# A Perceiver layer on one core: the last key's projection and stores moved, the time mixing's exponentials first, other banks for the last attention output

## The chip, the core and the metric

The kernel runs on one core of a Trainium2 chip, in one launch. A core has a matrix engine (TensorE; PE in the profile, PEld for its weight loads), a vector engine (VectorE, DVE), a scalar engine (ScalarE, ACT), GpSimd (POOL) and SyncE (SP), which issues this kernel's DMAs. Each engine takes its instructions in order; semaphores order them across engines. The metric is the device time of one execution in microseconds (us), lower is better. Times are medians of several runs; one execution is recorded by the profiler.

## What is computed

All values are float32. `x` is [32, 64, 256]: 32 samples, 64 queries of 256 values. `ctx` is [32, 1601, 192]: 1601 context rows, so 1601 keys, in each sample. The layer is

```python
# cross attention, 16 heads of 64
xn = layernorm(x)
q  = heads(xn @ w_q)                 # [32, 16, 64, 64]
k, v = heads(ctx @ w_kv)             # [32, 16, 1601, 64] each
p  = softmax(q @ k.T / 8)            # over the 1601 keys
x  = x + heads_joined(p @ v) @ w_out + b_out
# time mixing, per sample over its 64 queries
xn = layernorm(x); s = xn moved by one query
k, v, r = (xn*m + s*(1-m)) @ W.T     # three mixes m, three weights Wk, Wv, Wr
td = exp(-exp(time_decay)); e = exp(time_first + k)
wkv_t = (num + e_t v_t) / (den + e_t);  num = td num + exp(k_t) v_t;  den = td den + exp(k_t)
x  = x + (sigmoid(r) * wkv) @ Wo.T + bo
# feed forward
x  = x + relu(layernorm(x) @ w1 + b1) @ w2 + b2
```

The last line stands for the feed-forward part, which the change does not touch.

## The kernel before

**Folding.** Keys and values of the 1601 rows are never formed. Each head's query is folded with its part of `Wk`, so that a score is the product of a folded query (192 values) and a context row. The weighted sum of context rows is taken first and projected with `Wv` afterwards. Of the 1601 keys, 1536 lie in 12 blocks of 128, the next 64 are the rest block, and the last one (number 1600, the "odd" key) is handled by itself.

**Setup stage** (0 to about 142 us). `Wk` is transposed head pair by head pair (`wkT_ps`, L399 and L400). Then four groups `tg` of eight samples follow. Each group is worked in two halves `e` of eight heads: the queries (`q_ps`, L282, copied with the scale by ScalarE to a slice of `room[1]`), the folded queries' first 128 values (`ql_ps`, L300, and `q_lo`, L307) and their last 64 (`qh_ps`, L322). They are stored to `q_dram` (L310, L336). The odd key's context rows `codn` are transposed to `cod` (`cod_ps`, L217) and projected to all heads (`kod_ps`, L224, copied to `kodT`) once, behind the second half of the first group. `odd_scores` (L242) makes that key's scores after both halves of each group, and four small stores for each half send them to `o_dram` (L254). Their source is `od`: for the first half a tile that borrows the memory of `m2` (named `spare`), for the second a slice of `room[1]`.

**Memory that is used twice.** `room[0]` and `room[1]` are the two buffers of the tag `s_sb`. In the setup stage they hold weights and queries; later they hold the scores of the half batches in turn. `room[0]` becomes the scores of u = 0 and `room[1]` those of u = 1. The tile `m2` becomes the running maximum of the scores.

**Half batches.** After the setup 64 half batches follow, u = 0 to 63: sample b and half j of its heads, 512 columns (8 heads of 64 queries). For each u:

- for j = 0 the rest block's scores (`rest_ps`, L616, copied at L627), with the odd key's row read back from `o_dram`;
- the scores: 72 matmuls into six tiles `s_ps` of two PSUM banks (L639), ScalarE copies each tile to `s_sb` (L646), VectorE forms the maximum `m` (L648, L650), GpSimd takes it over the partitions (`mb`, L663);
- `av_lo` and `av_hi` of the half batch before: `o_lo` (48 matmuls at L449) and `o_hi` (48 at L847), begun and ended by the rest block's `left` (L797, L807), in PSUM banks with the tags `o_lo` and `o_hi`;
- `exps(u)`: `left` first (VectorE subtracts the maximum from `rest` at L671, ScalarE takes the exponential at L672, and SP stores the odd key's row of it to `pd_dram`), then three parts of four blocks (L682, L683);
- `total` and `inverse` of the denominators (`t` L759, GpSimd's `den` L762, VectorE's `turned` L774 and `rden`), and `out`, which multiplies `o_lo` and `o_hi` by them into `oT_lo` and `oT_hi` (L868, L873).

**Other work in between.** Every four half batches complete two samples, 128 rows, which is one of 16 tiles i. With phase = (u - 5) % 4: phase 0 projects to values (`Out.vproj`; it also multiplies the odd key's weights with its values, `odd`, L895, whose inputs SP loads as `odd_pd`), phase 1 projects the output (`yproj`) and norms, phase 2 mixes (`mix`), and phase 3 does the time mixing's projections. A dictionary `fill` puts such work behind a matmul c of `av_lo`: in phase 3 `project` stands behind c = 3 and `gate` behind c = 9.

```python
elif phase == 3 and i >= 0:
    fill = {3: [mixer.project], 9: [mixer.gate]}
```

`project` makes `Wk_ps` and `Wv_ps` on TensorE and then, on ScalarE, `ek` (L533) and two instructions `e` (L535); `gate` makes `Wr_ps`. All three go by a helper whose line is L449. In u = 3 the same place holds the odd key's values for all samples (`odd_values`: `vod`, L704 and L712), its outputs (`odd_outs`: `u_ps`, L723), and `decay`.

**What sets the order.** A scheduler orders each engine's instructions by the program's order and by `tc.issue_after(x)`, which holds what is issued under it until instruction `x` stands in the order. The DMAs' order on SP is decided in the same way, and each DMA issue waits for the DMA that was issued eight before it. Behind the last group's stores, SP loads for u = 0 the `rest` rows, `rows`, the second sample's `cb`, folded queries `q`, the first sample's context `c` (L143), and then `late_loads` (`wv_lo` and the other weights, from L419).

Of the kernel before, what the change touches and what calls it, by code (L numbers as in the profile page):

```python
# [9 lines left out]
F32 = mybir.dt.float32  # L10
# [10 lines left out]
def kernel(  # L21
# [104 lines left out]
    with ExitStack() as st_b:  # L126
        with ExitStack() as st_a:
# [83 lines left out]
                    copied = nc.vector.tensor_copy(xnT[:, c, :], pt)  # L211
                return xnT, copied

            def last_keys(codn, wk_lo, wk_hi, kodT, sps):

                pc = sps.tile([P, 2, B], F32, tag="ps", name="cod_ps")
                nc.tensor.transpose(pc[:, 0, :], codn[:, 0:P], ident[0:B, 0:B])  # L217
                nc.tensor.transpose(pc[0:C2, 1, :], codn[:, P:C], ident[0:B, 0:B])
                nc.vector.tensor_copy(cod[:, 0, :], pc[:, 0, :])
                nc.vector.tensor_copy(cod[0:C2, 1, :], pc[0:C2, 1, :])  # L220
                pk = sps.tile([P, NP, B], F32, tag="ps", name="kod_ps")
                for n, w, rs in ((0, wk_lo, slice(0, P)), (1, wk_hi, slice(0, C2))):
                    for hp in range(NP):
                        nc.tensor.matmul(  # L224
                            pk[:, hp, :],
                            lhsT=w[:, hp * P : (hp + 1) * P],
                            rhs=cod[rs, n, :],
                            start=(n == 0 and hp == 0),
                            stop=(n == 1),
                            skip_group_check=True,  # L230
                        )
                nc.vector.tensor_copy(kodT, pk)

            def odd_scores(tg, e, kodT, qTs, od, sps):

                po = [
                    sps.tile([P, TG], F32, tag="f", name=f"odd_ps_{tg}_{e}_{o}", bufs=6)
                    for o in range(2)
                ]
                for k in range(4):  # L240
                    for o in range(2):
                        nc.tensor.matmul(  # L242
                            po[o][k * B : (k + 1) * B, :],
                            lhsT=kodT[o * HD : (o + 1) * HD, 4 * e + k, :],
                            rhs=qTs[k // 2][o * HD : (o + 1) * HD, k % 2, :],
                            start=True,
                            stop=True,
                        )
                nc.vector.tensor_copy(od[:, 0, :], po[0])
                nc.scalar.copy(od[:, 1, :], po[1])  # L250
                for k in range(4):
                    r0 = k * B + tg * QB
                    h0 = 8 * e + 2 * k
                    nc.sync.dma_start(  # L254
                        o_dram[tg][h0 : h0 + 2].rearrange("o b n -> b o n"), od[r0 : r0 + QB]
                    )

            def queries(tg, xnT, copied, sp, sps, wq_sb, wkT, room, kodT, codn, wk_lo, wk_hi, spare):

                more = tg + 1 < B // QB
                following = None, None
                all_q = []
                for e in range(NP // 4):
                    if e == 0 and more:
                        with tc.issue_after(copied.ins):
# [3 lines left out]
                    for g in (2 * e, 2 * e + 1):  # L272
                        slot = (tg * NP // 2 + g) % 5
                        qT = room[1][:, slot * 2 * TG : (slot + 1) * 2 * TG].rearrange(
                            "p (k t) -> p k t", k=2
                        )
                        qTs.append(qT)
                        for k in range(2):
                            hp = 2 * g + k
                            pq = sps.tile([P, TG], F32, tag="ps", name=f"q_ps_{tg}_{hp}")  # L280
                            for c in range(2):
                                nc.tensor.matmul(  # L282
                                    pq,
                                    lhsT=wq_sb[:, c, hp * P : (hp + 1) * P],
                                    rhs=xnT[:, c, :],
                                    start=(c == 0),
                                    stop=(c == 1),
                                )
                            nc.scalar.activation(qT[:, k, :], pq, AF.Copy, scale=HD**-0.5)
                    if e == 1 and more:  # L290
                        following = turned_x(tg + 1, xn, sp, sps)
                    for g, qT in zip((2 * e, 2 * e + 1), qTs):
# [21 lines left out]
                    all_q.append(qTs)  # L314
# [19 lines left out]
                    for n in range(2):  # L334
# [2 lines left out]
                            q_dram[tg][:, P:C, ns].rearrange("b p n -> p b n"),  # L337
                            hi[n * C2 : (n + 1) * C2].rearrange("p b h t -> p b (h t)"),
                        )
                    if e == 1 and tg == 0:  # L340
                        last_keys(codn, wk_lo, wk_hi, kodT, sps)
                    if e == 1:
                        for n in range(2):
                            odd_scores(tg, n, kodT, all_q[n], spare[n], sps)
                return following, store

            def ctx_prep(b):
# [12 lines left out]
            with tc.tile_pool(name="setup", bufs=1) as sp, tc.tile_pool(  # L360
# [19 lines left out]
                wkT = wkT.rearrange("p (h c) -> p h c", c=C)  # L380
                wqr = w_q.rearrange("(c p) n -> p c n", p=P)
                halves = [slice(n * INNER // 2, (n + 1) * INNER // 2) for n in range(2)]
                for n, ns in enumerate(halves):
                    nc.sync.dma_start(wk_lo[:, ns], w_kv[0:P, ns])
                    nc.sync.dma_start(wk_hi[:, ns], w_kv[P:C, ns])
                    if n == 0:
                        nc.sync.dma_start(x_sb[:, 0:2, :], xr[:, 0:2, :])
                        nc.sync.dma_start(x_sb[:, 2:4, :], xr[:, 2:4, :])
                for ns in halves:
                    nc.sync.dma_start(wq_sb[:, :, ns], wqr[:, :, ns])  # L390
                for n in range(4, NT, 4):
                    nc.sync.dma_start(x_sb[:, n : n + 4, :], xr[:, n : n + 4, :])
                nc.sync.dma_start(codn, ctx_768[:, NK - 1, :])
                b_tiles = {0: blocks_load(0)}
                for g in range(NP // 2):
                    ps = sps.tile([P, 2, C], F32, tag="ps", name=f"wkT_ps_{g}")
                    for k in range(2):
# [3 lines left out]
                            ps[:, k, P:C], wk_hi[:, hp * P : (hp + 1) * P], ident[0:C2, 0:C2]  # L401
                        )
                    nc.scalar.copy(wkT[:, 2 * g : 2 * g + 2, :], ps)

                turned = turned_x(0, normed_x(0, sp), sp, sps)
                for tg in range(B // QB):
                    turned, store = queries(tg, *turned, sp, sps, wq_sb, wkT, room, kodT, codn, wk_lo, wk_hi, spare)
# [69 lines left out]
            class Mixing:  # L477
# [48 lines left out]
                def project(self):  # L526
# [5 lines left out]
                    self.e = rp.tile(shape, F32, tag="e", name=f"e_{i}")  # L532
                    nc.scalar.activation(self.ek, pk, AF.Exp)  # L533
                    for c in range(2):
                        nc.scalar.activation(  # L535
                            self.e[:, c], pk[:, c], AF.Exp, bias=cols[:, 1, c : c + 1]
                        )
                    self.ekv = rp.tile(shape, F32, tag="in_v", name=f"ekv_{i}")
# [199 lines left out]
            class Half:  # L738
# [85 lines left out]

                def av_lo(self, fill, behind):

                    self.po = ps_o.tile([P, HALF], F32, tag="o_lo", name=f"o_lo_{self.u}")
                    self.ph = ps_o.tile([P, HALF], F32, tag="o_hi", name=f"o_hi_{self.u}")[:, 0:HH]
# [50 lines left out]
            class Out:  # L879
# [7 lines left out]
                def vproj(self):  # L887
# [6 lines left out]
                    self.odd = rp.tile([ODD, P], F32, tag="odd", name=f"odd_{i}")  # L894
                    nc.vector.tensor_tensor(self.odd, odd_pd[:, 0], odd_pd[:, 1], ALU.mult)  # L895
                    pv = [bank([P, 2, 2, P], f"v_ps_{i}_{r}") for r in range(2)]
                    for r in range(2):
                        for j in range(2):
# [24 lines left out]
                                    )  # L923
                    for r in range(2):
                        nc.scalar.copy(self.outT[:, :, r], pv[r])

                def yproj(self):
                    i = self.i
# [20 lines left out]
            for u in range(2 * B):  # L949
# [12 lines left out]
                    turned_w = []  # L962
                elif u == 3:
                    fill = {
                        3: [lambda: vods.append(odd_values())],
                        6: [lambda: odd_outs(vods[0])],
                        9: [lambda: decay(top)],
                    }
                    vods = []
                elif phase == 1 and i >= 0:  # L970
                    fill = {2: [out.yproj], 6: [older.out] if i else []}
                elif phase == 2 and i >= 0:
# [5 lines left out]

                    hooks = {3: parts[0:2], 4: parts[2:3], 5: parts[3:]}
                elif last is not None:  # L980
                    hooks = {3: [last.inverse]}
                    last.total()
                else:
                    hooks = {}
# [9 lines left out]
                if last is not None:  # L994
                    last.av_lo(fill, done)
                parts = exps(u, s_sb, rests[j], mb)
                with tc.issue_after(turned_w[-1].ins) if u == 2 else ExitStack():
                    for part in parts if u else ():
                        part()
                if u == 1:  # L1000
# [30 lines left out]
            last.out()  # L1031
            older.scan()
            out.vproj()
            out.yproj()

        NB = 4
# [128 lines left out]
```

## Time and profile before

| | us |
|---|---|
| median of 3 runs | 2641.41 |
| range of the runs | 2638.94 to 2643.0 |
| the profiled execution's own time | 2641.73 |
| its span (first to last instruction) | 2639.9 |
| TensorE busy in it | 2576.9 |
| VectorE busy | 1928.4 |
| ScalarE busy | 984.6 |
| GpSimd busy | 409.7 |

The mean granted clock of TensorE in that execution is 0.986 of full speed. The profile names instructions by engine, line and tile; in the lists of waits, the columns are the total in us, the number of times, and the longest. In the timelines, the first number is the start from the span's beginning and the second the length; the bracket at the end gives the idle time just before and what ended it. In the tables of windows there follow for each stretch the length, the busy time of each engine (with the number of instructions), the granted clock, the share of the DMA engines and GB/s.

### The profile page before, as it was taken

How to read it: one execution, taken by the hardware profiler on the slowest of the kernel's cores; microseconds unless marked ns; L12 is line 12 of the kernel's file. 1: busy time of each engine (PE TensorE's matmuls, PEld its weight loads, DVE VectorE, ACT ScalarE, POOL GpSimd, SP SyncE). 2: the span in 40 equal slices, each digit the busy share in tenths (PEclk: the TensorE clock that was granted, in tenths of full speed). 3: DMA queues.
4: the chain of work that ended last, by engine and by line, in shares of the span. 5: the costliest groups of instructions: out<-in, count | busy, mean ns of one | idle time of the engine just before them, and what ended most of it. 6: DMA issues, size and time to landing. Idle time of an engine off the chain costs nothing.

```text
span 2639.9 us, 38243 instructions
## 1 busy us (share of the span) xinstructions
PE 2576.9 (98%) x15650; PEld 1236.6 (47%) x15650; DVE 1928.4 (73%) x2363; ACT 984.6 (37%) x1104; POOL 409.7 (16%) x372
## 2 busy tenths in 40 slices
PE   8989999999999999999999999999999999999999
PEld 4334444444444444444444444444444444444466
DVE  4466777878787878878787878878787878787631
ACT  2343334434333434333433334343343334343221
POOL 1001111111111111111111111111111111111100
PEclk9999999999999999999999999999999999999999
DMA  7885332333232223233233222323332322310100
GB/s 175 233 211 82 73 65 45 64 64 63 53 64 57 53 51 64 46 64 64 54 63 61 58 50 53 65 45 65 64 61 55 64 56 50 55 45 2 51 11 22
DMA packets 435968, 174.24 MB, mean 66 GB/s; under 512 B 334960, under 2 KB 421520, under 8 KB 435792
## 3 DMA queue, kind: packets, MB, share of 16 engines
q1 hardware_dynamic: 435792, 171.79, 31.6%
q8 instruction: 123, 2.02, 0.3%
q14 instruction: 53, 0.43, 0.1%
HBM read 141.07 MB, written 29.10 MB: 64 GB/s over the span
## 4 chain that ended last, share of the span: by engine, by line
PE 66%; DVE 14%; issue 11%; POOL 4%; ACT 3%; SPq 2%; DMA 1%; DVEq 0%; POOLq 0%; ACTq 0%
PE s_ps L639 27%; PE o_lo L449 14%; PE o_hi L847 8%; DVE s_sb L682 4%; DVE m L650 3%; PE y_ps L449 2%; PE q_ps L282 2%; DVE t L759 2%; PE h_ps L1076 2%; PE fy L1090 2%; POOL mb L663 2%; POOL den L762 2%; PE ql_ps L300 1%; DVE cT L355 1%; PE v_ps L902 1%
## 5 line engine op out<-in xcount | busy, mean ns | idle before, releaser
L639 PE MATMUL s_ps<-q,cT 64*128 64x512 f32 x4608 | 1006.6, 591 | 3.7 <-ACT rest L627 2.3
L449 PE MATMUL o_lo<-s_sb,c 128*64 128x512 f32 x3072 | 709.6, 609 | 6.8 <-DMA c<-in_ctx_dram 6.8
L639 PEld LDWEIGHTS s_ps<-q,cT 64*128 64x128 f32 x4608 | 442.2, 187 | 535.6 <-issue 518.2
L646 ACT COPY s_sb<-s_ps 128x1024 f32<-128x1024 f32 x384 | 388.5, 1012 | 732.8 <-PE s_ps L639 731.1
L682 DVE TENSOR_TENSOR s_sb<-s_sb,mb 128x2048 f32<-128x2048 f32 x192 | 431.5, 2283 | 0.0
L683 ACT ACTIVATE s_sb<-s_sb 128x2048 f32<-128x2048 f32 x192 | 367.3, 1914 | 124.3 <-DVE s_sb L682 124.3
L449 PEld LDWEIGHTS o_lo<-s_sb,c 128*64 128x64 f32 x3072 | 218.5, 140 | 403.9 <-issue 399.6
L650 DVE TENSOR_TENSOR m<-m,s_sb 128x1024 f32<-128x1024 f32 x256 | 312.3, 1220 | 47.7 <-ACT s_sb L646 27.1
L847 PE MATMUL o_hi<-s_sb,c 128*64 128x256 f32 x3072 | 342.8, 379 | 0.0
L759 DVE TENSOR_TENSOR t<-t,s_sb 128x1024 f32<-128x1024 f32 x256 | 311.9, 1218 | 8.7 <-DVE rstd_ln L110 0.4
L847 PEld LDWEIGHTS o_hi<-s_sb,c 128*64 128x64 f32 x3072 | 222.3, 137 | 139.2 <-issue 38.4
L762 POOL PARTITION_ALL_REDUCE den<-t x64 | 207.1, 3236 | 387.3 <-issue 365.9
L774 DVE STREAM_TRANSPOSE turned<-den 128x512 f32<-128x512 f32 x64 | 45.5, 711 | 274.5 <-POOL den L762 274.5
L672 ACT ACTIVATE rest<-rest 128x512 f32<-128x512 f32 x64 | 40.4, 631 | 504.8 <-DVE rest L671 485.7
L663 POOL PARTITION_ALL_REDUCE mb<-m x64 | 114.2, 1785 | 469.2 <-DVE m L656 414.9
L671 DVE TENSOR_TENSOR rest<-rest,mb 128x512 f32<-128x512 f32 x64 | 44.3, 692 | 108.4 <-POOL mb L663 108.4
L604 POOL MEMSET rest<- 64x256 f32 x128 | 39.3, 307 | 428.7 <-issue 192.9
L355 DVE STREAM_TRANSPOSE cT<-cb 128x768 f32<-128x768 f32 x96 | 89.5, 957 | 9.0 <-DMA cb<-in_ctx_dram 9.0
L797 PE MATMUL o_lo<-rest,rows 64*128 64x256 f32 x256 | 82.8, 404 | 4.2 <-DVE oT_lo L868 4.2
L648 DVE TENSOR_TENSOR m<-s_sb 128x1024 f32<-128x1024 f32 x64 | 76.2, 1191 | 12.1 <-DMA o_dram<-spare 12.0
L807 PE MATMUL o_hi<-rest,rows 64*128 64x256 f32 x256 | 83.0, 405 | 0.0
L111 POOL TENSOR_TENSOR rstd_ln<-rstd_ln,root 128x1 f32<-128x1 f32 (+1 forms) x24 | 32.1, 1337 | 313.0 <-DVE rstd_ln L110 287.3
(156 smaller groups left out, 1837.7 us busy)
## 6 DMA issues: line engine op xcount, KB each, us to landing
q<-q_dram SPq DMA_DIRECT2D x64, 768.0 KB
c<-in_ctx_dram SPq DMA_DIRECT2D x32, 1152.0 KB
cb<-in_ctx_dram SPq DMA_DIRECT2D x192, 104.0 KB
cb<-in_ctx_dram SPq DMA_DIRECT2D x192, 96.0 KB
q_dram<-q_lo SPq DMA_DIRECT2D x16, 1024.0 KB
q_dram<-q_hi SPq DMA_DIRECT2D x16, 512.0 KB
rest<-o_dram SPq DMA_DIRECT2D x128, 1.0 KB
rows<-in_ctx_dram SPq DMA_DIRECT2D x64, 32.0 KB
```

Source lines behind the costliest of these rows:

```text
L355: nc.vector.transpose(cT[:, s, 0 : NB1 * BL], c[:, s, 0:NB1, :])
L449: last = nc.tensor.matmul(out[rs], lhsT=lhsT[:, rs], rhs=rhs, start=start, stop=stop, skip_group_check=True,)
L639: done = nc.tensor.matmul(ps[:, k, :], lhsT=cT[rs, s, i * P : (i + 1) * P], rhs=q[rs, s, js : js + HALF], start=(s == 0), stop=(s == NS - 1),)
L646: copied = nc.scalar.copy(s_sb[:, 2 * i : 2 * i + 2, :], ps)
L650: nc.vector.tensor_tensor(m2, m2, s_sb[:, 2 * i : 2 * i + 2, :], ALU.max)
L663: nc.gpsimd.partition_all_reduce(mb, mx, P, bass_isa.ReduceOp.max)
L682: nc.vector.tensor_tensor(s, s, m, ALU.subtract)
L683: nc.scalar.activation(s, s, AF.Exp)
L759: nc.vector.tensor_tensor(t2, t2, p[:, 2 * i : 2 * i + 2, :], ALU.add)
L762: nc.gpsimd.partition_all_reduce(self.den, t2[:, 0, :], P, bass_isa.ReduceOp.add)
L807: nc.tensor.matmul(self.ph, lhsT=self.rows.rearrange("p n c -> p (n c)")[hi, c0 : c0 + P], rhs=self.rest[hi, (1 - k) * HH : (2 - k) * HH], ...
L847: nc.tensor.matmul(self.ph[o * C2 : (o + 1) * C2, :], lhsT=self.ctx[:, self.at[c], P:C], rhs=self.s_sb[:, c, o * HH : (o + 1) * HH], start ...
```

## The change

1. `codn` is the first load on SP, and `cod` is made ahead of the weights' transposes. The projection to `kodT` is a function of its own, `projected_keys(e)`, for half of the heads: half 0 stands behind the second of the four groups of weight transposes, half 1 in the first group behind its first queries. Both use PSUM banks of the tag `f`.
2. `odd_scores` is called once in each half, between the `q_lo` and the `q_hi` part, and the stores are a function `odd_store`. For the last group both halves' `od` are slices of `room[1]`, and the eight stores are kept in the list `odd_late` and issued in u = 0 ahead of `late_loads`, behind the load of `c`.
3. In u = 3, `decay` stands behind c = 3 and `odd_values` behind c = 9; `odd_outs` moves to u = 4.
4. `odd` leaves `vproj` for `share`, called in phase 1 by a hook behind the fourth copy of the scores.
5. In phase 3 `exps(u)` is issued after the last exponential of `project`.
6. The last half batch's `o_lo` and `o_hi` are two banks of a score tile (tag `s`) in place of the banks of the tags `o_lo` and `o_hi`.

```diff
-            def last_keys(codn, wk_lo, wk_hi, kodT, sps):
-                pc = sps.tile([P, 2, B], F32, tag="ps", name="cod_ps")
+            def last_keys(codn, sps):
+                pc = sps.tile([P, 2, B], F32, tag="f", name="cod_ps", bufs=6)
...
-                pk = sps.tile([P, NP, B], F32, tag="ps", name="kod_ps")
+            def projected_keys(e, wk_lo, wk_hi, kodT, sps):
+                hps = range(4 * e, 4 * e + 4)
+                pk = sps.tile([P, 4, B], F32, tag="f", name=f"kod_ps_{e}", bufs=6)
...
-                nc.vector.tensor_copy(kodT, pk)
+                nc.vector.tensor_copy(kodT[:, 4 * e : 4 * e + 4, :], pk)
...
+                    if e == 0 and tg == 0:
+                        projected_keys(1, wk_lo, wk_hi, kodT, sps)
...
+                    od = spare[e]
+                    if not more and e == 0:
+                        slot = (tg * NP // 2 - 1) % 5
+                        od = room[1][:, slot * 2 * TG : (slot + 1) * 2 * TG].rearrange(
+                            "p (o t) -> p o t", o=2
+                        )
+                    odd_scores(tg, e, kodT, qTs, od, sps)
+                    if more:
+                        odd_store(tg, e, od)
+                    else:
+                        odd_late.append(lambda e=e, od=od: odd_store(tg, e, od))
...
-                    if e == 1 and tg == 0:
-                        last_keys(codn, wk_lo, wk_hi, kodT, sps)
-                    if e == 1:
-                        for n in range(2):
-                            odd_scores(tg, n, kodT, all_q[n], spare[n], sps)
...
+                nc.sync.dma_start(codn, ctx_768[:, NK - 1, :])
                 for n, ns in enumerate(halves):
...
-                nc.sync.dma_start(codn, ctx_768[:, NK - 1, :])
                 b_tiles = {0: blocks_load(0)}
+                odd_late = []
+                last_keys(codn, sps)
...
+                    if g == 1:
+                        projected_keys(0, wk_lo, wk_hi, kodT, sps)
...
-                        nc.scalar.activation(
+                        self.exps = nc.scalar.activation(
                             self.e[:, c], pk[:, c], AF.Exp, bias=cols[:, 1, c : c + 1]
...
+                    if self.u < 2 * B - 1:
...
+                    else:
+                        both = ps_s.tile([P, 2, HALF], F32, tag="s", name=f"o_{self.u}")
+                        self.po, ph = both[:, 0, :], both[:, 1, :]
...
+                def share(self):
+                    self.odd = rp.tile([ODD, P], F32, tag="odd", name=f"odd_{self.i}")
+                    nc.vector.tensor_tensor(self.odd, odd_pd[:, 0], odd_pd[:, 1], ALU.mult)
...
                     fill = {
-                        3: [lambda: vods.append(odd_values())],
-                        6: [lambda: odd_outs(vods[0])],
-                        9: [lambda: decay(top)],
+                        3: [lambda: decay(top)],
+                        9: [lambda: vods.append(odd_values())],
                     }
...
+                elif u == 4:
+                    fill = {6: [lambda: odd_outs(vods[0])]}
...
-                    hooks = {3: [last.inverse]}
+                    hooks = {3: [last.inverse] + ([out.share] if phase == 1 and i >= 0 else [])}
...
-                with tc.issue_after(turned_w[-1].ins) if u == 2 else ExitStack():
+                ahead = turned_w[-1] if u == 2 else mixer.exps if phase == 3 and i >= 0 else None
+                with tc.issue_after(ahead.ins) if ahead else ExitStack():
...
+                        for work in odd_late:
+                            work()
                         late_loads()
```

More of the change, by code (lines that the diff above doesn't have):

```diff
@@ L220, in last_keys @@
                 nc.vector.tensor_copy(cod[0:C2, 1, :], pc[0:C2, 1, :])
-                pk = sps.tile([P, NP, B], F32, tag="ps", name="kod_ps")
+            def projected_keys(e, wk_lo, wk_hi, kodT, sps):
+                hps = range(4 * e, 4 * e + 4)
+                pk = sps.tile([P, 4, B], F32, tag="f", name=f"kod_ps_{e}", bufs=6)
                 for n, w, rs in ((0, wk_lo, slice(0, P)), (1, wk_hi, slice(0, C2))):
-                    for hp in range(NP):
+                    for hp in hps:
                         nc.tensor.matmul(
-                            pk[:, hp, :],
+                            pk[:, hp - 4 * e, :],
                             lhsT=w[:, hp * P : (hp + 1) * P],
                             rhs=cod[rs, n, :],
-                            start=(n == 0 and hp == 0),
+                            start=(n == 0 and hp == 4 * e),
                             stop=(n == 1),
@@ L250, in odd_scores, with odd_store @@
                 nc.scalar.copy(od[:, 1, :], po[1])
+            def odd_store(tg, e, od):
                 for k in range(4):
@@ L256, in odd_scores, with queries @@
                     )
-            def queries(tg, xnT, copied, sp, sps, wq_sb, wkT, room, kodT, codn, wk_lo, wk_hi, spare):
+            def queries(tg, xnT, copied, sp, sps, wq_sb, wkT, room, kodT, wk_lo, wk_hi, spare):
                 more = tg + 1 < B // QB
                 following = None, None
-                all_q = []
                 for e in range(NP // 4):
@@ L313, in queries @@
                         )
-                    all_q.append(qTs)
+                    od = spare[e]
[9 more added lines that the diff above has]
+                        odd_late.append(lambda e=e, od=od: odd_store(tg, e, od))
                     for k in range(2):
@@ L403 @@
                     nc.scalar.copy(wkT[:, 2 * g : 2 * g + 2, :], ps)
+                    if g == 1:
+                        projected_keys(0, wk_lo, wk_hi, kodT, sps)
                 turned = turned_x(0, normed_x(0, sp), sp, sps)
                 for tg in range(B // QB):
-                    turned, store = queries(tg, *turned, sp, sps, wq_sb, wkT, room, kodT, codn, wk_lo, wk_hi, spare)
+                    turned, store = queries(tg, *turned, sp, sps, wq_sb, wkT, room, kodT, wk_lo, wk_hi, spare)
                     if tg == 1:
@@ L825, in av_lo @@
                 def av_lo(self, fill, behind):
-                    self.po = ps_o.tile([P, HALF], F32, tag="o_lo", name=f"o_lo_{self.u}")
-                    self.ph = ps_o.tile([P, HALF], F32, tag="o_hi", name=f"o_hi_{self.u}")[:, 0:HH]
+                    if self.u < 2 * B - 1:
+                        self.po = ps_o.tile([P, HALF], F32, tag="o_lo", name=f"o_lo_{self.u}")
+                        ph = ps_o.tile([P, HALF], F32, tag="o_hi", name=f"o_hi_{self.u}")
+                    else:
+                        both = ps_s.tile([P, 2, HALF], F32, tag="s", name=f"o_{self.u}")
+                        self.po, ph = both[:, 0, :], both[:, 1, :]
+                    self.ph = ph[:, 0:HH]
                     with tc.issue_after(behind.ins):
@@ L893, in vproj @@
                     self.outT = aw.tile([P, 2, 2, 2, P], F32, tag="outT", name=f"outT_{i}")
-                    self.odd = rp.tile([ODD, P], F32, tag="odd", name=f"odd_{i}")
-                    nc.vector.tensor_tensor(self.odd, odd_pd[:, 0], odd_pd[:, 1], ALU.mult)
                     pv = [bank([P, 2, 2, P], f"v_ps_{i}_{r}") for r in range(2)]
@@ L1033 @@
             out.vproj()
+            out.share()
             out.yproj()
```

## The prediction

> **What bounds the kernel now.** I read the page first, then TensorE's waits, then the timeline at each place that the change touches, and the granted clock in short windows.
>
> ```profile
> span 2639.9 us, 38243 instructions
> PE 2576.9 (98%) x15650; PEld 1236.6 (47%) x15650; DVE 1928.4 (73%) x2363; ACT 984.6 (37%) x1104; POOL 409.7 (16%) x372
> PE 66%; DVE 14%; issue 11%; POOL 4%; ACT 3%; SPq 2%; DMA 1%; DVEq 0%; POOLq 0%; ACTq 0%
> ```
>
> TensorE is busy for 98% of the span; 2639.9 - 2576.9 = 63.0 us are gaps. An edit can shorten the kernel by closing gaps, by raising the clock at which the same matmuls run, or by removing matmuls; it removes none. TensorE's waits list the gaps:
>
> ```profile
> PE Wr_ps L449 <- ACT e L535: 30.7, 14, 2.6
> PE o_lo L449 <- DMA c<-in_ctx_dram: 6.8, 1, 6.8
> PE o_lo L797 <- DVE oT_lo L868: 4.2, 1, 4.2
> PE kod_ps L224 <- DVE cod L219: 2.9, 1, 2.9
> PE u_ps L723 <- ACT vod L712: 2.6, 1, 2.6
> PE rest_ps L616 <- ACT room L250: 0.9, 1, 0.9
> ```
>
> Columns: total us, times, longest. Half of all gap time is one wait met 14 times: the matmuls into `Wr_ps` wait for ScalarE's exponentials `e`. ScalarE's timeline shows why:
>
> ```profile
> 451.42 0.63 ACT L672 ACTIVATE rest<-rest 128x512 f32<-128x512 f32 x1 [10.58 <-DVE rest L671]
> 451.95 0.36 ACT L533 ACTIVATE ek<-Wk_ps 128x256 f32<-128x256 f32 x1
> 452.22 0.62 ACT L535 ACTIVATE e<-Wk_ps,cols 128x128 f32<-128x128 f32 x2
> ```
>
> It idles 10.58 us for VectorE's `rest`, then does `ek` and `e`, whose input (`Wk_ps`, matmuls at 443.63) has been ready since about 445. The clock follows the gaps; windows after two `Wr_ps` gaps (ninth number: granted clock):
>
> ```profile
> 599.00:602.00 3.00, 3.00 (x14) 1.24 (x12) 3.00 (x4) 2.68 (x2) 0.00 (x0) 0.50 0.02 5
> 1040.00:1043.00 3.00, 3.00 (x30) 1.71 (x30) 3.00 (x4) 2.14 (x2) 0.00 (x0) 1.00 0.00 0
> ```
>
> Ten of the 14 gaps are followed by a stretch of 3.41 us at 0.50, four are not.
>
> **1. Exponentials first (steady state).** `ek`, `e`, `e` move ahead of the rest exponential: they can run at 445 to 446.5, well before `Wr_ps` is due at 450.7 (452.89 less its 2.19). All 14 gaps close: 30.7 us. VectorE's `rest` still comes at 451.4, when ScalarE is free, so neither the softmax nor its two small stores on SP are delayed. From the `odd` product at 440.5 to the one at 2348.1 lie 13 periods of four half batches, 1907.6 us, mean 146.74. TensorE's own periods are 147.05 with a half-clock stretch and near 145.7 without, 1.35 apart. Without gap and stretch: 146.74 - 2.19 - 10/13 x 1.35 = 143.5. ScalarE's copies of the rest scores have 0.65 us of slack at 498, so I give back 0.2: 143.7. The gain is 13 x 3.04 = 39.5, with the 14th gap (2.1) **41.6**. Bounds: 44 (30.7 + 10 x 1.35) and 18.7 (first rival).
>
> [...]
>
> **2. Last key projected in the setup stage.** Now it stands in the middle of the queries:
>
> ```profile
> 38.66 0.24 PE L217 MATMUL cod_ps<-ident,room 32*128 32x32 f32 x1
> 41.80 6.55 PE L224 MATMUL kod_ps<-cod,room 128*128 128x32 f32 x32 [2.87 <-DVE cod L219]
> 48.28 5.91 PE L282 MATMUL q_ps<-xnT,room 128*128 128x512 f32 x8
> ```
>
> Transposes 0.27, wait 2.87, matmuls 6.55 (32 records, 0.205 each), and the clock stays at 0.50 until 52.8, which costs the queries some 2.2: 11.8 us go. The same 32 records come back among the weights' transposes, before 13 us, at the half-clock price they have here: 6.55, plus 0.3 for the transposes and 0.5 because the key is now SP's first load: 7.4. The idle 0.54 and 0.77 that TensorE has there at 7.66 and 8.88 can hide 0.8 of it; 6.6 on the path. VectorE's two extra copies and its `q_lo` copies may hold TensorE 0.7 later on, and the 0.9 before `rest_ps` goes, its ScalarE copy now being far ahead: 11.8 - 6.6 - 0.7 + 0.9, about **5** gained (2 if nothing is hidden and each copy is waited for, 8 if the DMA arrivals set the head anyway).
>
> **3. Last stores behind loads.** The 12.0 us that VectorE's `m` waits for the store of `spare` go, but that wait hides today: `m` cannot end before the last score copy of that half. In its place comes a wait on ScalarE. For the last tile group the rows lie in a slice of `room`, the memory that becomes the `s_sb` of u = 1, so its first copy must wait for all eight late stores, and these are issued behind `c`:
>
> ```profile
> 140.79 5.11 SPq L336 DMA_DIRECT2D q_dram<-q_hi  x2
> 146.00 6.53 SPq L254 DMA_DIRECT2D o_dram<-spare  x4
> 152.64 1.43 SPq L254 DMA_DIRECT2D o_dram<-room  x4
> 169.60 0.60 SPq L143 DMA_DIRECT2D c<-in_ctx_dram  x1
> ```
>
> Each SP issue waits for the DMA eight issues before it, so the eighth store waits for `c` itself. `c` is issued at 169.6 and lands at 182.5; without eight stores ahead of it SP runs some 5 us earlier (its next lanes still wait for `q_hi`, landed at 153.6), so `c` lands near 177.4, the last store near 179.4. The copy that runs at 162.5 today runs at 179.5. Behind it on ScalarE queue the other copies of u = 1 and the exponentials of u = 0; TensorE fills the free score banks and stops from 164.8 to 180.5, then runs 3.41 us or more at half clock (2.7 us). The second scores end at 193.5 instead of 175.2. Today's 6.81 wait for `c` before av(0) (182.61) is absorbed, so the path loses 194.1 - 182.6 = 11.5, of which u = 2 sees about 10; the later `cb(2)` and `cT(1)` on SP add up to 3. I take **12 lost** (6 if half of the store traffic clears with `c`'s first half, 17 if nothing is absorbed).
>
> **4. Its values a half batch later.** TensorE's 2.59 wait for `vod` goes, because `u_ps` is now a half batch behind, and the half-clock stretch at 271.2 (1.7 us) with it: **4.3** gained; 2.6 if the clock drops for another gap. `odd`, split from the value projection, keeps its place on VectorE in every full period, so its 43.9 us of DMA waits stay: nothing.
>
> **5. Other banks at the end.** The last half batch takes score banks, free since its last copy at 2459, and no longer waits for VectorE's `oT_lo`:
>
> ```profile
> 2479.40 0.96 PE L797 MATMUL o_lo<-rest,rows 64*128 64x256 f32 x2 [4.17 <-DVE oT_lo L868]
> 2480.29 1.97 PE L449 MATMUL o_lo<-s_sb,c 128*64 128x512 f32 x2
> ```
>
> The wait is 4.17; behind it the clock is 0.50 from 2479.6 to 2486.5, and this av takes 24.35 us (2479.40 to 2503.75) against 19.7 of a usual one. Its exponentials end at 2472.5, so nothing else is late. 4.17 + 4.65 = 8.8 at most, 4.2 if the clock drops all the same; **8** taken.
>
> **Sum.** -41.6 - 5 + 12 - 4.3 - 8 = -46.9 on the profiled 2641.7 (span 2639.9 and 1.8 around it; the median 2641.4 lies 0.3 below): 2594.8, **2595**.
>
> **Rivals.**
> VectorE and GpSimd bind the period (0.17). In the three later periods without a half-clock stretch VectorE waits for no score copy and the period is still 145.2 to 145.4. If that is VectorE's own round, with its 9 us waits for GpSimd's `den`, the gap merely moves: 13 x (146.74 - 145.3) = 18.7 instead of 41.6, 2618. For it: VectorE waits 274.5 us for `den` in all. Against it: in the phase where that wait is 9 us, the reduction begins about 7 us after a memset that waits for TensorE's last `o_hi`, so the chain starts earlier when TensorE does.
> The half-clock stretches stay (0.06): if they follow something other than the gaps, 13.5 and the tail's 4.6 are lost, 2612. Against it: none occurs in a steady period outside the place behind a gap.
> The late stores are early (0.10): if SP's lanes clear by 160, the copy isn't held and the 12 turn into about -2: 2581.
> The order on ScalarE has no effect (0.04): `e` could be late for another reason, as a `Wk_ps` that VectorE or a PSUM bank delays; then step 1 gives nothing, 2637. Against it: `ek` and `e` run back to back behind `rest` with no wait of their own.
> Slower (0.03): the late stores land one after another, each queued behind the bytes of `c`, `cb` and the weights, and ScalarE's first copy of u = 1 waits for the eighth. The other steps gain 58.9, so this decides from 58.9 / 8 = 7.4 us a store. If each takes the 12.9 us of `c` (169.6 to 182.5), the eighth lands near 280, the stall is 118 and the kernel 59 slower, 2701. Against it: today's eight are issued within 8 us and land within 2.2 us of each other, 153.6 to 155.8.
>
> **How the numbers follow.** The forecast has 0.60. The sum of the good ends is -44 - 8 + 6 - 4.3 - 8.8 = -59, 2583, and the early stores reach 2577: the low end. The sum of the bad ends is -18.7 - 2 + 17 - 2.6 - 4.2 = -10.5, 2631; I end at 2628, leaving out the last two rivals and the worst of the bad ends together. A measurement of this kernel tells about 0.2% (5.3 us) from no change. Faster 0.93, with the ineffective order split between faster and same; same 0.03; slower 0.04.
>
> **What would show it.** Right: no `Wr_ps` wait for `e` and no half-clock stretch in the steady periods, 143.7 from one `odd` product to the next; `kod_ps` before 15 us and `q_ps` without a gap behind `ql_ps` near 39; a ScalarE copy waiting some 15 us for a DMA of `o_dram` between 160 and 185, TensorE idle with it; no wait for `oT_lo` near the end. Wrong: a period of 145 with VectorE free of waits on ScalarE (first rival); stores that land before 165; a new gap of TensorE in every period, which none of my steps contains.

## The result, and the profile after

The changed kernel takes 2603.41 us (median of 4 runs, 2602.06 to 2604.92) against 2642.2 before (2638.94 to 2644.06, 4 runs): a ratio of 0.9855, 95% interval 0.9838 to 0.9872, 38.8 us faster. The forecast was 2595, 47 faster. The profiled execution took 2602.79, its span 2601.0.

The page's span, busy line and chain of the kernel after:

```profile
span 2601.0 us, 38247 instructions
PE 2556.5 (98%) x15650; PEld 1224.4 (47%) x15650; DVE 1929.2 (74%) x2364; ACT 982.8 (38%) x1104; POOL 411.5 (16%) x372
PE 76%; DVE 10%; issue 5%; ACT 3%; POOL 2%; DMA 2%; SPq 2%; DVEq 0%; ACTq 0%; POOLq 0%
```

TensorE runs the same 15650 matmuls, 20.4 us faster (2576.9 to 2556.5). That is nearly all clock: the granted clock was 0.50 for 86.9 us of the span before and for 48.4 after, and half of this difference is 19.2. In both figures the start is counted (15.2 and 24.5 us), for which the trace has no record of the clock: in the kernel before transposes begin every 0.21 us there, and every 0.11 at clock 1.00 (33.83 to 34.04). TensorE's gaps shrank by 18.5 (63.0 to 44.5). Its waits now (total, times, longest):

```profile
PE s_ps L655 <- ACT s_sb L662: 20.3, 2, 15.1
PE s_ps L655 <- ACT rest L643: 9.1, 18, 0.9
...
PE qh_ps L339 <- ACT q_lo L315: 1.7, 1, 1.7
...
PE ql_ps L307 <- ACT q_lo L315: 1.2, 1, 1.2
PE rest_ps L632 <- ACT q_hi L348: 0.8, 1, 0.8
```

The waits for `e`, `vod`, `oT_lo` and `c` are gone. Two long waits for a ScalarE score copy (15.1 and 5.1) have come in, and 18 short ones for ScalarE's `rest` copies in place of 7.

Marks that both traces have split the difference by stage. Each number is the start after minus the start before:

| mark | before | after | difference | share of this stage | forecast |
|---|---|---|---|---|---|
| rest scores of u = 0 | 142.74 | 146.30 | +3.56 | setup +3.6 | -5 |
| rest scores of u = 2 | 200.48 | 213.23 | +12.75 | late stores +9.2 | +12 |
| rest scores of u = 8 | 422.24 | 433.27 | +11.04 | values later -1.7 | -4.3 |
| rest scores of u = 62 | 2403.95 | 2374.35 | -29.60 | steady state -40.6 | -41.6 |
| last value projection | 2503.75 | 2464.88 | -38.87 | last banks -9.3 | -8 |
| end of the span | 2639.87 | 2601.01 | -38.86 | 0 | 0 |

**Steady state.** ScalarE's timeline at the place shown before, in the same half batch:

```profile
455.77 0.38 ACT L549 ACTIVATE ek<-Wk_ps 128x256 f32<-128x256 f32 x1 [3.88 <-PE Wk_ps L465]
456.05 0.62 ACT L551 ACTIVATE e<-Wk_ps,cols 128x128 f32<-128x128 f32 x2
462.41 0.63 ACT L688 ACTIVATE rest<-rest 128x512 f32<-128x512 f32 x1 [5.74 <-issue]
```

`e` is done 4.9 us before `Wr_ps` is due at 461.58. From the `odd` product at 451.53 to the one at 2320.91 lie 13 periods of 143.80; 143.7 was forecast.

**Late stores.** SP, ScalarE and TensorE in u = 1:

```profile
167.19 0.60 SPq L143 DMA_DIRECT2D c<-in_ctx_dram  x1
167.84 13.18 SPq L260 DMA_DIRECT2D o_dram<-room  x8
```
```profile
182.70 1.93 ACT L662 COPY s_sb<-s_ps 128x1024 f32<-128x1024 f32 x2 [18.16 <-DMA o_dram<-room]
```
```profile
183.76 12.84 PE L655 MATMUL s_ps<-q,cT 64*128 64x512 f32 x48 [15.13 <-ACT s_sb L662]
```

The chain is the forecast one: the eighth store waits for `c` (SP waits 3.1 for it, and issues the store at 180.76), the copy for the store, TensorE for the copy. Counted from the rest scores of u = 0, the copy starts after 36.4 us; the forecast was 36.8.

### The profile page after: what moved, and what is told of

It is laid out like the page before. It is cut to its first block, busy times and chain, and to the rows that moved or that the text cites. A ratio compares the mean times of both kernels' runs of the same rounds, so it can differ in the third digit from the quotient of the medians.

```text
span 2601.0 us, 38247 instructions
## 1 busy us (share of the span) xinstructions
PE 2556.5 (98%) x15650; PEld 1224.4 (47%) x15650; DVE 1929.2 (74%) x2364; ACT 982.8 (38%) x1104; POOL 411.5 (16%) x372
## 4 chain that ended last, share of the span: by engine, by line
PE 76%; DVE 10%; issue 5%; ACT 3%; POOL 2%; DMA 2%; SPq 2%; DVEq 0%; ACTq 0%; POOLq 0%
PE s_ps L655 30%; PE o_lo L465 21%; PE o_hi L868 8%; DVE s_sb L698 4%; PE y_ps L465 2%; PE q_ps L287 2%; PE h_ps L1105 2%; PE fy L1119 2%; DVE m L666 2%; POOL den L778 1%; ACT rest L643 1%; PE ql_ps L307 1%; DVE t L775 1%; SPq L170 1%; PE o_lo L813 1%
## 5 line engine op out<-in xcount | busy, mean ns | idle before, releaser
L465 PE MATMUL o_lo<-s_sb,c 128*64 128x512 f32 x3024 | 677.1, 595 | 0.0
L465 PEld LDWEIGHTS o_lo<-s_sb,c 128*64 128x64 f32 x3024 | 208.5, 137 | 380.1 <-issue 375.8
L868 PE MATMUL o_hi<-s_sb,c 128*64 128x256 f32 x3024 | 337.0, 379 | 0.0
L790 DVE STREAM_TRANSPOSE turned<-den 128x512 f32<-128x512 f32 x64 | 45.5, 712 | 247.9 <-POOL den L778 247.9
L620 POOL MEMSET rest<- 64x256 f32 x128 | 39.3, 307 | 299.7 <-PE o_lo L813 150.1
```

Of the source, the lines that this page charges most:

```text
L465: last = nc.tensor.matmul(out[rs], lhsT=lhsT[:, rs], rhs=rhs, start=start, stop=stop, skip_group_check=True,)
L868: nc.tensor.matmul(self.ph[o * C2 : (o + 1) * C2, :], lhsT=self.ctx[:, self.at[c], P:C], rhs=self.s_sb[:, c, o * HH : (o + 1) * HH], start ...
```

## Experiments

All times are medians beside runs of the kernel before on the same chip (2641.8 to 2642.3).

**1. Only the exponentials first, on the kernel before.**

```diff
-                        nc.scalar.activation(
+                        self.exps = nc.scalar.activation(
...
-                with tc.issue_after(turned_w[-1].ins) if u == 2 else ExitStack():
+                ahead = turned_w[-1] if u == 2 else mixer.exps if phase == 3 and i >= 0 else None
+                with tc.issue_after(ahead.ins) if ahead else ExitStack():
```

> The kernel before with only the order on ScalarE changed in phase 3 (ek, e, e ahead of the rest exponential). Theory: TensorE bounds the period; all 14 waits for e go and with them ten half-clock stretches, 143.8 us from one odd product to the next in place of 146.7, in all 39 to 43 us faster, 2600 us. Rival (VectorE and GpSimd bind the period): 145.3 a period, 19 faster, 2623. Rival (the stretches do not hang on these gaps): about 29 faster, 2613, with ten stretches at 0.50 still there. The head, the waits for c and for vod and the last wait for oT_lo stay as they were.

Measured: 2603.02, ratio 0.9854 (0.984 to 0.9867), 39.3 faster. This one edit brings as much as the whole change; the other parts together bring about nothing. In TensorE's waits the old ones stand, without the one for `e`:

```profile
PE s_ps L639 <- ACT rest L627: 9.2, 19, 0.8
PE o_lo L449 <- DMA c<-in_ctx_dram: 6.9, 1, 6.9
PE o_lo L797 <- DVE oT_lo L868: 4.2, 1, 4.2
```

The 9.2 for `rest` (2.3 before) is the give-back: 7 us in all, 0.5 a period, where 0.2 had been allowed. No steady period has a half-clock stretch left; the mean granted clock is 0.993 (before: 0.986). The first rival (VectorE binds, 2623) is out, and so is the one by which the stretches stay.

**2. Only the values later and the last banks, on the kernel before.**

```diff
-                        3: [lambda: vods.append(odd_values())],
-                        6: [lambda: odd_outs(vods[0])],
-                        9: [lambda: decay(top)],
+                        3: [lambda: decay(top)],
+                        9: [lambda: vods.append(odd_values())],
...
+                elif u == 4:
+                    fill = {6: [lambda: odd_outs(vods[0])]}
...
+                        both = ps_s.tile([P, 2, HALF], F32, tag="s", name=f"o_{self.u}")
+                        self.po, ph = both[:, 0, :], both[:, 1, :]
```

> The kernel before with two far-apart parts of the change: the odd key's values at c = 9 of u = 3 with its outputs in u = 4, and the last half batch in score banks. Theory: the 2.6 wait for vod and the 4.2 wait for oT_lo go with their half-clock stretches. The last part brings 9 us between the rest scores of u = 62 and the last value projection. The first part, between the rest scores of u = 2 and u = 6, brings 4 to 6: in the kernel after this stretch was only 1.7 shorter than before, but with a wait of 5.1 for a score copy in it that I put down to the late stores, so without them 6.8 less. Together 13 to 16 faster, 2627. Rival (the wait of 5.1 belongs to the move of the values): only 2 for the first part, 2631.

Measured: 2629.09, ratio 0.9954 (0.994 to 0.9968), 13.2 faster. By marks: 5.3 between the rest scores of u = 2 and u = 8, and 9.3 at the end. So the move of the values does bring what was forecast (4.3). In the kernel after, the late stores' second wait hides most of it: from u = 2 to u = 8 it takes 216.4 here and 216.5 in experiment 3, which has this move without the late stores, against 220.0 in the kernel after and 221.8 before.

**3. The kernel after with the last group's stores at once.**

```diff
-                    if not more and e == 0:
...
-                    if more:
-                        odd_store(tg, e, od)
-                    else:
-                        odd_late.append(lambda e=e, od=od: odd_store(tg, e, od))
+                    odd_store(tg, e, od)
```

With this the first half's rows also go back to the tile `spare`.

> The kernel after with the last group's stores issued at once, as in the other groups, and the first half's rows again in the tile spare in place of a slice of room. Theory: the 18.2 wait of ScalarE's copy for the stores of o_dram and TensorE's 15.1 go, the half-clock stretch from 171 to 188 with them; the wait for c of some 7 comes back ahead of the first weighted sum. From the rest scores of u = 0 to those of u = 2 it takes 58 in place of 67, and the 5.1 wait at 260 goes too: 9 + 5 = 14 faster than the kernel after, 2589. Rival (the bytes of the queries' stores hold the copy or c anyway): within 3 us of the kernel after, 2601 to 2603.

Measured: 2590.58, ratio to before 0.9806 (0.9792 to 0.9819), 12.8 faster than the kernel after. Both waits for a score copy have left TensorE's waits, and the one for `c` is back:

```profile
PE s_ps L647 <- ACT rest L635: 9.1, 23, 0.9
PE o_lo L457 <- DMA c<-in_ctx_dram: 8.4, 1, 8.4
```

From the rest scores of u = 0 to those of u = 2 it takes 59.9 (after: 66.9; before: 57.7). The stores behind the loads, with the buffer that goes with them, are a pure loss of 13.

**4. Only the last key moved, on the kernel before.**

```diff
+                nc.sync.dma_start(codn, ctx_768[:, NK - 1, :])
                 for n, ns in enumerate(halves):
...
+                last_keys(codn, sps)
...
+                    if g == 1:
+                        projected_keys(0, wk_lo, wk_hi, kodT, sps)
...
+                    if e == 0 and tg == 0:
+                        projected_keys(1, wk_lo, wk_hi, kodT, sps)
```

> The kernel before with only the last key moved: codn first on SP, cod ahead of the weights' transposes, its projection in two halves amid them; the odd key's scores stay together at the end of each group. In the kernel after the rest scores of u = 0 began 3.6 later than before, where 5 earlier had been forecast. Theory A (the clock): the narrow projection matmuls of 32 columns and the transposes do not raise the clock, so full clock begins 9 later (24.5 in place of 15.2), and the head gains only 11.8 - 7.4 - 1.0 = 3.4: rest scores at 139.3, 2639. The rest of the loss in the kernel after then lies in the halved odd scores. Theory B (the head alone loses it): rest scores at 145 to 146, 2645.

Measured: 2638.12, ratio 0.9985 (0.9977 to 0.9994), 4.2 faster; the rest scores of u = 0 begin at 139.58. Theory A holds in its time and in the begin of full clock (24.82); theory B's 145 to 146 is out. The same mark is 144.04 with the odd key's scores halved (experiment 3) and 146.30 with the late stores' buffers as well (the kernel after).

These are single executions, and one difference between them is luck: the time at which full clock begins. Kernels with the same head differ by more than 1 us in it. The kernel before and experiments 1 and 2 have one setup stage, and this mark is at 142.74, 144.25 and 142.24. With the new head the 16 query matmuls that begin at 20.5 take 9.25 here, 8.20 in experiment 3 and 9.08 in the kernel after.

So halving the scores costs 4.5 by the marks and 5.5 without this luck. The traces of experiments 3 and 4 show where: the odd key's 128 matmuls take 8.71 in place of 7.79 (16 in a row take 1.09, 32 take 1.95), the 128 into `ql_ps`, which the new order interleaves with others in a different way, 37.04 in place of 34.45, and TensorE waits 1.9 for `q_lo` copies that experiment 4 doesn't wait for. Of the last 2.3, 1.0 is the begin of full clock (it is there at the first odd scores, 33.23 against 32.23), and 1.2 is a longer wait for the last `q_lo` copies (1.69 in place of 0.52), which wait for a store; why that store is later was not traced.

**5 and 6. The narrow matmuls in one piece, or in four, among wide ones.** Both start from the kernel before, with `codn` and `cod` early. In one piece:

```diff
+                    if e == 1 and tg == 0:
+                        with tc.issue_after(asked.ins):
+                            projected_keys(0, wk_lo, wk_hi, kodT, sps)
+                            projected_keys(1, wk_lo, wk_hi, kodT, sps)
```

In four, `projected_keys` is a generator that yields behind every eight matmuls:

```diff
                             nc.scalar.activation(qT[:, k, :], pq, AF.Copy, scale=HD**-0.5)
+                            with tc.issue_after(asked.ins):
+                                next(pieces, None)
```

> The kernel before with codn and cod early, and all 32 narrow projection matmuls in one piece behind the queries of the first group's second half, in front of eight transposes. TensorE waits for nothing there. Theory (a stretch of narrow matmuls and transposes counts as idle for the clock): half clock begins within 3.4 us of the piece although there is no gap, and stays for one or two stretches of 3.41; rest scores of u = 0 at 142.7 - 3.1 - 2.6 + 0.5 = 137.5, less what the two stretches of before (10.2 us at 0.50) shorten to, 136 to 138; 2637. Rival (only gaps lower the clock): no half clock between 20 and 140, rest scores at 134 to 135, 2634.

> As the kernel with one piece, but the 32 narrow matmuls in four pieces of eight, one behind each pair of wide query matmuls. Theory: no stretch of 3.41 us is mostly narrow, so the clock stays at 1.00 from its first rise near 17; the projection costs 32 x 0.123 = 3.9 in place of 6.55, its wait 2.87 and the half clock behind it (about 2.2) go, SP's first load costs 0.5: rest scores at 135 to 136, 7 faster than before, 2635, and 1 to 3 faster than in one piece. Rival (only gaps lower the clock): the same time as in one piece.

Measured: 2636.59 in one piece (0.9978, 0.9968 to 0.9987) and 2635.4 in four (0.9973, 0.9964 to 0.9983). The times alone don't tell them apart. One more execution of the one-piece kernel gave the profile (2637.95):

> The kernel with all 32 narrow matmuls in one piece once more, for a profile. Theory (narrow matmuls and transposes count as idle for the clock): a half-clock stretch begins within 3.4 us of the piece without any gap of TensorE, rest scores of u = 0 at 136 to 138. Rival: clock 1.00 from its first rise to the wait for c.

TensorE's timeline and windows there (ninth number: granted clock):

```profile
35.82 4.79 PE L228 MATMUL kod_ps<-cod,room 128*128 128x32 f32 x32
40.54 0.47 PE L208 MATMUL xnT_ps<-ident,xn_in_k 128*128 128x128 f32 x1
...
42.44 4.41 PE L308 MATMUL ql_ps<-room,room 64*128 64x512 f32 x12
```
```profile
36.00:38.00 2.00, 2.00 (x19) 1.92 (x18) 0.17 (x1) 0.60 (x1) 0.00 (x0) 1.00 0.97 241
38.00:40.00 2.00, 2.00 (x14) 1.96 (x14) 0.12 (x1) 0.00 (x0) 0.00 (x0) 0.70 0.07 25
40.00:42.00 2.00, 2.00 (x10) 1.94 (x11) 0.60 (x2) 0.00 (x0) 0.00 (x0) 0.50 0.00 0
```

TensorE is busy all the time and the clock falls to 0.50, 3.0 us after the first narrow matmul, and stays there for 6.8. In four pieces, the same work in the same place:

```profile
34.00:38.00 4.00, 4.00 (x20) 2.31 (x18) 0.00 (x0) 1.14 (x2) 0.00 (x0) 1.00 0.60 147
38.00:42.00 4.00, 4.00 (x24) 2.24 (x23) 3.24 (x11) 0.05 (x1) 0.00 (x0) 1.00 0.00 0
```

The rest scores of u = 0 begin at 139.03 and 136.08. Of these 3.0, 1.6 are there before the first narrow matmul: the queries of the second half begin at 28.85 and 27.30, because full clock began at 18.33 and 15.68. The pieces themselves save 1.4, and the medians, 1.2 apart, agree.

**7. All good parts.** The kernel before with experiments 1, 2 and 6; the odd scores and their stores as before.

> The kernel before with the exponentials first, the odd key's values a half batch later, the last banks, and the projection in four pieces among wide matmuls; the odd key's scores together at the end of each group and the stores as before. If the parts add up: 2642.2 - 39.3 - 13.2 - 7 = 2583; 7 faster than the kernel after with its stores at once (2590.6). If the parts share a bound (VectorE): 2590.

Measured: 2581.64, ratio 0.9771 (0.9757 to 0.9786): 60.5 faster than before and 21.8 faster than the kernel after. The parts add up (39.3 + 13.2 + 6.7 = 59.2).

**8 and 9. The first `c` earlier,** on that kernel, either ahead of the second sample's blocks, or in the setup stage.

```diff
                     with tc.issue_after(store.ins):
+                        if b == 0:
+                            c_tiles[b] = ctx_load(b)
                         b_tiles[b + 1] = blocks_load(b + 1)
```

```diff
                         q_tiles = {0: q_load(0)}
+                        early_c = ctx_load(0)
```

> As the kernel with all good parts, and the first context tile c loaded ahead of the second sample's blocks cb. Theory: c lands some 8 to 10 us earlier, so TensorE's wait for c (7 to 8 us) ahead of the first weighted sum goes with the half clock around it (some 10 us at 0.50, 3 to 5 us lost): 9 to 12 faster than without, 2572. Rival (the second sample's blocks become the late ones, or the last stores hold the DMA queues): the wait moves to the scores of u = 2, within 3 of it, 2581.

> The kernel with all good parts, and the first context tile c loaded in the setup stage, behind the folded queries of the second group, in place of behind the second sample's blocks. Theory: TensorE's wait for c (7.1) goes with the stretch of 6.8 us at half clock behind it (3.4 lost), and since cb and q of the second sample are no longer behind c, nothing takes its place: 9 to 11 faster than all good parts without it, 2572. Rival (the setup stage's stores fill the DMA engines, so 1.15 MB more there delays q_lo's and q_hi's buffers): the setup ends some 5 later, 2577, or the same time.

Measured: 2581.35 (0.9771, 0.9756 to 0.9785) and 2582.53 (0.9773, 0.9759 to 0.9786): no gain. The wait of 7.1 for `c` is gone in both, and other waits have come in. First the kernel with `c` ahead of the blocks, then the one with `c` in the setup stage:

```profile
PE rest_ps L627 <- DMA cT<-cT: 8.8, 1, 8.8
```
```profile
PE s_ps L651 <- ACT rest L639: 15.1, 26, 4.4
PE rest_ps L628 <- DMA cT<-cT: 3.2, 1, 3.2
```

In the first, the stretch from the rest scores of u = 0 to those of u = 2 is as long as without the edit (58.1 against 58.0). In the second it is 5.5 shorter (52.5), but the setup stage ends 2.7 later (138.31 against 135.63) and the stretch from u = 2 to u = 8 is 5.5 longer (224.4 against 218.9). So `c` alone is not what is late; that the transfers behind the setup stage as a whole are, the two runs suggest, and which bytes could be spared was not tried.

## Why the prediction was right

The direction and the main term were right, and the time lies in the range. The forecast was 8 us too low, which is part 2's miss of 8.6; by the table above the others (2.8 better, 2.6 worse, 1.0 worse, 1.3 better) cancel, and that is luck.

**Part 1, the exponentials.** 41.6 forecast, 40.6 between marks, 39.3 alone. Both halves of the term held: the gaps (30.7) and the half-clock stretches (ten of 3.41 us before; in the kernel after the clock is 1.00 from 263.5 to 2471.9). The reason given against the rival, that GpSimd's reduction starts with TensorE and moves with it, was not tested by itself; it agrees with VectorE's waits for `den`, which fell from 274.5 to 247.9 when the period shrank.

**Part 2, the last key.** This step failed: 5 gained was forecast, 3.6 was lost. What the prediction priced was about right: with the projection alone moved, the rest scores of u = 0 come 3.2 earlier, and the time is 4.2 shorter (experiment 4). The queries begin 7.4 later (20.59 against 13.17); 6.6 had been taken. What it did not cost at all are the halved odd scores: 5.5 (experiments 3 and 4). The diff showed them; the prediction priced what moved out of the queries and not what moved in. With the late stores' buffer comes the longer wait of 1.2 for `q_lo`, also not costed.

The last 1.0 is luck of the clock. Full speed begins at 24.54 in place of 15.22, but mostly because the queries begin later: in the kernel before and experiments 1 and 2 it begins 2.1 to 4.1 us behind the first query matmul, in the kernel after and experiments 3 and 4 2.2 to 4.3 us. The 16 query matmuls take 9.08 in place of 8.13 (and 7.13 at full clock), as the second of these rows of the kernel after shows; in experiment 3, with the same head, they take 8.20:

```profile
8.38 5.17 PE L228 MATMUL kod_ps<-cod,room 128*128 128x32 f32 x22 [0.76 <-DVE cod L219]
...
20.59 9.08 PE L287 MATMUL q_ps<-xnT,room 128*128 128x512 f32 x16
```

The first row also shows a sign that came only in part: 22 of the `kod_ps` matmuls run before 15 us, but eight begin at 16.15 and two at 20.03.

**Part 3, the late stores.** 12 lost was forecast, between 6 and 17. In u = 0 and u = 1 it is 9.2 against the kernel before. Taking the late stores and their buffer away gives 12.8; between the marks of the two profiles that is 2.3 in the setup stage (1.0 of it the clock's luck above), 7.0 from u = 0 to u = 2, 3.5 from u = 2 to u = 8, and 1.1 behind. So the size came out, but not all of it where it was forecast. The 3.5 come from the second wait:

```profile
260.33 12.11 PE L655 MATMUL s_ps<-q,cT 64*128 64x512 f32 x48 [5.13 <-ACT s_sb L662]
```

The prediction had this only as "up to 3" for `cb(2)`. ScalarE's exponentials of u = 2 (to 259.4) are still running when the scores of u = 3 want their copies, since VectorE had fallen behind in u = 1. The wait is 5.1 and the 3.4 us at half clock that follow cost 1.7; against this, 6.8 us at half clock behind the `vod` matmuls of experiment 3 (3.4 lost) are absent here (in experiment 2 the second half of these and the `o_lo` and `o_hi` behind them take 12.62 us, here 9.26), which leaves 3.4.

**Part 4, the values.** 4.3 forecast; 5.3 when done alone, 1.7 in the kernel after. `odd` kept its place: its waits for DMA are 40.7 us in 14 waits, against 43.9 in 15.

**Part 5, the last banks.** 8 forecast, 9.3 measured, in the kernel after and in experiment 2 alike:

```profile
2445.47 0.38 PE L813 MATMUL o<-rest,rows 64*128 64x256 f32 x1
...
2446.00 3.65 PE L465 MATMUL o<-s_sb,c 128*64 128x512 f32 x16
```

The upper bound of 8.8 was itself 0.5 short.

## What to carry to other kernels

A wait that recurs in a loop is worth its length and the clock that it costs (here 30.7 us in 14 gaps, and ten stretches of 3.41 us at 0.50), and an order of two instructions on an engine that is idle two thirds of the time can be all of a change's gain: look first at what the waiting engine waits *behind*. A store moved "out of the way" still holds its source buffer (ScalarE's copy waited 18.16 us for it here); find who takes that memory next, and count the queue from there. When a block of work is moved, cost the place that it moves into as carefully as the place that it leaves.

## What the runs showed of the clock

Wherever the traces before and after record the granted clock, it is 1.00 or 0.50. The stretches at 0.50 last 3.41 us, or 6.83, 10.24 and 17.07, which are two, three and five times that. The length of a gap did not decide what followed it. The 14 `Wr_ps` gaps of the kernel before are 2.09 to 2.62 us long; the longest, up to 1627.12, left the clock at 1.00, and the shortest, up to 1185.01, was followed by 0.50 from 1185.99 to 1189.40. A gap of 1.80 us, in front of `xT_ln` at 2508.88, was followed by 0.50 too (2510.36 to 2513.77). So in this loop one and the same wait cost a half-clock stretch ten times and none four times; what decides between the two was not shown. Nor was it shown whether the spread of experiment 2's runs, which have these gaps (2620.95 to 2630.88; the kernel after, without them, 2602.06 to 2604.92), comes of this.

A gap was not needed. 32 matmuls of 32 columns with eight transposes behind them were followed by 0.50 without one (experiment 5: 0.70 in the window from 38 to 40 us, 0.50 from 40 to 44); in four pieces among matmuls of 512 columns the clock stayed at 1.00 from 30 to 42 (experiment 6). The 32 matmuls into `vod_ps` have 32 columns too, and run in one piece without a gap. In the kernel before they run from 257.86 to 262.30, and the clock is 0.50 from 260.98 to 267.80; in the kernel after they run from 281.53 to 285.41, and it stays at 1.00 (windows from 278 to 302). What makes the difference was not shown.

In the head of the kernel after, the transposes and 30 of these narrow matmuls keep TensorE busy from 8.4 to 20.0 at half pace (a transpose every 0.21 us, at 43.21 to 43.43 every 0.11), and full clock begins at 24.54, 4.0 us behind the first wide matmul (2.2 and 4.3 in experiments 3 and 4).
